# Cached keys of an attention layer turned on VectorE and through DRAM, in place of TensorE

## The chip, the cores and the metric

The kernel runs on one core of one Trainium2 chip, in fp32. The metric is the device time of one execution in microseconds (us). A core has five engines with an instruction stream each: TensorE (PE, matmuls and transposes; its weight loads are listed apart as PEld), VectorE (DVE), ScalarE (ACT), GpSimd (POOL) and SyncE (SP), which here only issues transfers. Each engine runs its own stream in order, and the streams meet at semaphores. Transfers run on 16 DMA engines beside them. SBUF and PSUM have 128 partitions.

## The reference

Four residual layers change x, 8 sequences of 128 tokens with 512 features. Layer 0 is a gated feed-forward net with low-rank adapters and then a mixture of 8 low-rank experts, layer 1 an adapter and experts, layer 3 experts chosen by language and 64 small experts. Layer 2, where the change lies, is attention with a paged cache, then experts:

```python
q = jnp.einsum('bsd,ed->bse', x, Wq).reshape(bsz, seqlen, HQ, D)   # HQ = 32, D = 128
k = jnp.einsum('bsd,ed->bse', x, Wk).reshape(bsz, seqlen, HK, D)   # HK = 8
v = jnp.einsum('bsd,ed->bse', x, Wv).reshape(bsz, seqlen, HK, D)
q, k = _rope(_rmsnorm(q, q_norm_w), pos), _rope(_rmsnorm(k, k_norm_w), pos)
kc = k_cache[block_table].reshape(bsz, L, HK, D)   # 16 pages of 32 rows: L = 512
vc = v_cache[block_table].reshape(bsz, L, HK, D)
k_all, v_all = concatenate([kc, k]), concatenate([vc, v])   # 512 cached + 128 new
scores = where(valid, einsum('bqhd,bkhd->bhqk', q, k_all) / sqrt(D), -1e30)
o = einsum('bhqk,bkhd->bqhd', softmax(scores), v_all)
out = einsum('bse,de->bsd', o.reshape(bsz, seqlen, HQ * D), Wo)
```

Here `valid` hides the cached rows at and behind `cache_seqlens`.

## The kernel before

The activations x stay in SBUF, transposed: 128 partitions, 4 chunks of features, 1024 tokens. The whole program is one launch: layers 0 and 1 take the first 329 us of the profiled execution, then attention up to about 1460 us, then the rest of layer 2 and layer 3.

**The steps of attention.** There are 32 steps n = (qd, p) (L832): the 8 key heads qd outside, 4 pairs p of sequences inside. A step handles two sequences, j = 0 and 1, each with the 4 query heads of one key head. For a step the kernel

- gathers the cached keys and values, 128 rows to an indirect DMA, four for each j and kind, on POOL's queue (`gather`, L877 to L891). The row numbers are in `kvrow`, made once from the block table (L173 to L185). Chunk c of a sequence has cached rows 128c to 128c + 127 on its partitions;
- projects the new q, k and v (`project`, with `seven`, a Strassen-like product of seven small ones: L918 matmuls, L929 and L930 VectorE, L961 the adds that give q, v and k; the last of them is k's), rotates and norms them (`rotate`, `normed`: L990 on POOL, L994, L1018, L1022 on VectorE);
- turns the cached keys so that the head's 128 features lie on the partitions (`turn_cached`, L1025 to L1034): four PE transposes of 128x128 for each j into one PSUM tile `kTc` (L1032), then a VectorE copy into the SBUF tile `kT` (L1033). `kT` is 128 x 2 x 640, and the last 128 columns of each j take the new keys, turned and copied by `turn` (L1041, L1042), which also turns q (L1047, L1049);
- computes the scores, `st`, 5 chunks of keys against 512 columns of q (L53, called from `weigh`), and their exponentials `pT` on ScalarE with the mask as bias (L1061);
- adds up the five chunks on VectorE (`added`, L1072: four adds, the last makes `part`), sums that over the keys with a PE product against ones (`sum`, L1081), takes the reciprocal (L1087), copies it to R (L1089) and spreads R with three DMAs on SP (L1091, and one more at L1092);
- multiplies with the values (`mix`: `av` on PE, L53, then `oT` on VectorE, L1103), prepares the output product (`outputs`, L900, tiles `os`), and adds the product with Wo to y (`leave`: `seven` again with the tiles `wo_one`, `wo_two`, `wo_six`, and `uo` on VectorE at L929).

**The order.** `run` (L1163 to L1230) writes the steps out by hand, three of them in flight: while step n computes its scores, step n - 1 is finished and step n + 1 is projected, rotated and turned. In the loop body of step n: scores of j = 0 and their adds; `mix` of step n - 1, j = 1; divisors of j = 0; `outputs(n - 1)`; `project(n + 1)`; `leave(n - 1)` with `rotate(n + 1)` inside it; `normed(n + 1)`; the gathers of the values for n + 1; weights for a new qd or the token sums (`tokens`, L900, tile `xs`) of step n + 2; the output weights; scores of j = 1 and their adds; `mix` of j = 0; `turn_cached(n + 1)`; the divisors of j = 1; `turn(n + 1)`; the gathers of the keys for n + 2; and the factors of new weights (L858, tiles `q_s`). Instructions that are marked `kept` stay in this order on their engine once `run` has begun; the others are moved by the framework's scheduler. Before `run`, `begin` (L1148) starts step 0 while layer 1 computes: weights, key gathers, `turn_cached(0)`, the gathers of values and of the keys of step 1, and the first factors. In that stretch layer 1's x adds (L294) and its expert routing (L238 to L266, ending in `mw_l`, which PE turns as `midTp_l` at L277) run on VectorE.

Pools: `kn` (gathered keys), `kT`, `pT` and R have two buffers for each tile, `xs`, the rotated q and k and the parts one. PSUM has three buffers for the tag "mm" (`kTc`, `kTn`, `qTp`, `sum`, most of `seven`), three for "st" and two for "av". The rotary tables' small pool `rp` lives to the end of the program.

Of the kernel before, what the change touches and what calls it, by code (L numbers as in the profile page):

```python
# [10 lines left out]
F32 = mybir.dt.float32  # L11
I32 = mybir.dt.int32
AF = mybir.ActivationFunctionType
ALU = mybir.AluOpType
# [3 lines left out]
P = 128  # L18
# [29 lines left out]
def forward(ctx: ExitStack, tc: tile.TileContext, a: dict, out: bass.AP):  # L48
# [15 lines left out]
    wop = ctx.enter_context(tc.tile_pool(name="wop", bufs=1))  # L64
    rp = ctx.enter_context(tc.tile_pool(name="rp", bufs=1))

# [22 lines left out]
    sp.dma_start(x[:, :, 512:NT], a["xT"].rearrange("(c p) t -> p c t", p=P)[:, :, 512:NT])  # L89
    second = gate_weights(1)  # L90


# [41 lines left out]
    def rows(name, n, where=const):  # L134
# [37 lines left out]

    selp = w0.tile([P, NB * 4, 4], F32, tag="selp", name="selp")  # L173
    dve.tensor_tensor(
        selp,
        table.rearrange("p (c j) -> p c j", j=4),
        block32.unsqueeze(1).to_broadcast([P, NB * 4, 4]),
        ALU.mult,
    )
    page = const.tile([P, NB * 4], F32, tag="page", name="page")  # L180
    dve.tensor_reduce(page, selp, AX.X, ALU.add)
    dve.tensor_scalar(page, page, 32.0, p_mod32, ALU.mult, ALU.add)
    kvrow = const.tile([P, NQ, NB * 4], I32, tag="kvrow", name="kvrow")
    for qd in range(NQ):
        dve.tensor_scalar(kvrow[:, qd, :], page, float(NQ), float(qd), ALU.mult, ALU.add)  # L185

# [471 lines left out]
    with psa:  # L658
# [10 lines left out]

        att = attention(tc, a, x, ident, lens, kvrow, part, ww, wop, ypool, sums, rot, ps_, c2, chunks, mm)  # L670

# [80 lines left out]
    with tc.If(redo > 0):  # L752
        sp.dma_start(x, kept)
        y2 = attention_any(tc, a, x, ident, lens, kvrow, part, ww, wop, ypool, rot, rows, chunks, mm)
        with ExitStack() as c3:
# [21 lines left out]

def attention(tc, a, x, ident, lens, kvrow, part, ww, wop, ypool, sums, rot, psa, c2, chunks, mm):

# [10 lines left out]
    ap = c2.enter_context(tc.tile_pool(name="ap", bufs=1))  # L790
    trig, straight, crossed, eps = rot

# [39 lines left out]
    steps = [(qd, p) for qd in range(NQ) for p in range(NP)]  # L832
    S = {n: {} for n in range(len(steps))}
    W, WO = {}, {}

# [40 lines left out]
    def gather(n, what):  # L876
        qd, p = steps[n]  # L877
        t = []
        for j in range(2):
            if what == "k":  # L880
                d = kvp.tile([P, 4, HD], F32, tag="kn", name=f"kn_{n}_{j}")
            else:
                d = vals[n % 2 * 2 + j]
            for c in range(4):
                i = (2 * p + j) * 4 + c
                kept(pool.indirect_dma_start(  # L886
                    out=d[:, c, :], out_offset=None, in_=kc if what == "k" else vc,
                    in_offset=bass.IndirectOffsetOnAxis(ap=kvrow[:, qd, i : i + 1], axis=0),
                ))
            t.append(d)  # L890
        S[n][what + "c"] = t  # L891

# [132 lines left out]
    def turn_cached(n):  # L1025

        s = S[n]
        kT = wk.tile([P, 2, LK], F32, tag="kT", name=f"kT_{n}")
        for j in range(2):
            ps = psa.tile([P, 512], F32, tag="mm", name=f"kTc_{n}_{j}", bufs=3)  # L1030
            for c in range(4):
                pe.transpose(ps[:, c * P : (c + 1) * P], s["kc"][j][:, c, :], ident)  # L1032
            dve.tensor_copy(kT[:, j, 0:L], ps)  # L1033
        s["kT"] = kT  # L1034

    def turn(n):
# [3 lines left out]
        for j in range(2):  # L1040
            pe.transpose(ps[:, j, :], s["k"][:, j, 0, :], ident)  # L1041
        dve.tensor_copy(s["kT"][:, :, L:LK], ps)  # L1042
        qT = []
# [9 lines left out]
    def weigh(n, j):  # L1053

        s = S[n]
        b = 2 * steps[n][1] + j
        pT = wk.tile([P, NC, REP, P], F32, tag="pT", name=f"pT_{n}_{j}")
        for c in range(NC):
            ps = psa.tile([P, REP * P], F32, tag="st", name=f"st_{n}_{j}_{c}", bufs=3)
            mm(ps, s["kT"][:, j, c * P : (c + 1) * P], s["qT"][j], True, True)  # L1060
            act.activation(  # L1061
                pT[:, c, :, :].rearrange("p i t -> p (i t)"), ps, AF.Exp,
                bias=hide[:, b, c : c + 1] if c < 4 else 0.0,
            )
        return pT
# [97 lines left out]
    def run(pool_, end, bank):  # L1163
# [12 lines left out]
        for n, (qd, p) in enumerate(steps):  # L1176
# [8 lines left out]
            if after:  # L1185
                project(after)
                leave(n - 1, lambda: rotate(after))
            elif last:
                leave(n - 1)
# [16 lines left out]
            mix(n, 0, pT)  # L1206
            if n + 1 < len(steps):
                turn_cached(n + 1)
            divisors(n, 1)
# [25 lines left out]
def rotary(tc, rp, tp, lens, part, rows, kept):  # L1235
# [43 lines left out]

    eps = rp.tile([P, 1], F32, tag="eps", name="eps")  # L1280
    pool.memset(eps, EPS_RMS)
    return (trig, straight, crossed, eps), steps(), last


def attention_any(tc, a, x, ident, lens, kvrow, part, ww, wop, ypool, rot, rows, chunks, mm):
    nc = tc.nc
# [4 lines left out]
    with ExitStack() as c2:  # L1291
        rp = c2.enter_context(tc.tile_pool(name="rp", bufs=1))
        psa = c2.enter_context(tc.tile_pool(name="psa", bufs=2, space=PSUM))

        trig, straight, crossed, eps = rot

# [9 lines left out]
        wk = c2.enter_context(tc.tile_pool(name="wk", bufs=2))  # L1306

        kc = a["k_cache"].rearrange("g s (q h) d -> (g s q) (h d)", q=NQ)
        vc = a["v_cache"].rearrange("g s (q h) d -> (g s q) (h d)", q=NQ)
# [678 lines left out]
```

## The time and the profile before

| | |
|---|---|
| median of 6 runs | 1685.52 us (1685.16 to 1690.82) |
| the profiled execution: its time, its span | 1696.47 us, 1694.7 us |
| mean granted TensorE clock | 0.991 |
| PE busy before 329 us, 329 to 1460, after 1460 | 322.25, 1071.43, 218.42 us |
| `kTc` transposes on PE, 256 | 33.2 us, 273 ns each |
| copies `kT<-kTc` on VectorE, 64 | 41.1 us, 681 ns each |
| key gathers on POOL, 256 | 269.5 us, 1053 ns each |
| R transfers on SP, 192 | 64 KB each |
| DMA traffic | 94.41 MB, mean 56 GB/s |

All times inside come from the one profiled execution; a time such as 1143.42 is counted from the start of its span. A line of the timeline gives the start, the length, the engine, the line of the program, the operation with its output and inputs by name, the tile's shape and, in brackets, how long the engine had been idle before it and what ended that. A line of the groups gives the sum of the busy time, the mean in ns, and the idle time before with its releasers. A time of 37.3 us is the usual length of an attention step.

### The profile page before, as it was taken

Reading aid. Unit: us, or ns where it says so; the run is one execution under the profiler, and the core shown is the slowest. Engines: PE = TensorE matmul, PEld = TensorE weight load, DVE = VectorE, ACT = ScalarE, POOL = GpSimd, SP = SyncE. Lnnn points to the kernel's source line nnn. Section 1 sums busy time; section 2 is a strip of 40 time slices with the busy share of each in tenths; the row PEclk is TensorE's granted clock in tenths of the full one; section 3 lists DMA queues with packets and bytes.
Section 4 is the critical chain, followed back from the end, with each engine's and each line's share of the span. In section 5 each row is a group of like instructions: output and inputs, shape, how many; then the busy total and the mean of one; then the engine's idle time right before and its main releaser. Section 6 shows DMA issues by size and latency. Waiting matters only on the chain.

```text
span 1694.7 us, 19398 instructions
## 1 busy us (share of the span) xinstructions
PE 1612.1 (95%) x6561; PEld 984.9 (58%) x6561; DVE 1073.6 (63%) x2224; ACT 563.1 (33%) x1390; POOL 818.2 (48%) x778
## 2 busy tenths in 40 slices
PE   9999999999999999999999999999999999899998
PEld 7888875555555555555555555555455555458653
DVE  4665324777777767777676767777776767663141
ACT  1111000443433344433433344443443344330110
POOL 2242025456665565656665555666566566530000
PEclk9999999999999999999999999999999999999899
DMA  8110011112121211212121211112121211202001
GB/s 291 38 44 10 1 44 53 66 38 79 45 64 44 72 35 60 74 36 65 44 77 38 67 56 51 60 39 80 40 65 44 74 35 60 84 23 79 0 13 39
DMA packets 69194, 94.41 MB, mean 56 GB/s; under 512 B 16800, under 2 KB 40544, under 8 KB 68960
## 3 DMA queue, kind: packets, MB, share of 16 engines
q1 hardware_dynamic: 50944, 56.09, 10.5%
q0 software_dynamic: 17056, 36.49, 7.0%
q8 instruction: 54, 0.88, 0.2%
q10 hardware_dynamic: 1088, 0.52, 0.1%
q14 instruction: 52, 0.43, 0.1%
HBM read 76.14 MB, written 4.33 MB: 47 GB/s over the span
## 4 chain that ended last, share of the span: by engine, by line
PE 89%; DVE 6%; issue 2%; POOL 1%; ACT 1%; another core or an unknown queue 1%; DVEq 0%; ACTq 0%; POOLq 0%
PE av L53 16%; PE st L53 15%; PE g L356 7%; PE q_six L918 7%; PE q_one L918 5%; PE wo_two L918 5%; PE q_five L918 5%; PE dn L356 4%; PE wo_one L918 3%; PE wo_six L918 3%; PE eo_l L53 2%; PE z L53 2%; PE h L1557 2%; PE qTp L1047 2%; PE o L53 2%
## 5 line engine op out<-in xcount | busy, mean ns | idle before, releaser
L53 PE MATMUL st<-qT,kT 128*128 128x512 f32 x640 | 296.1, 598 | 14.7 <-ACT pT L1061 11.6
L886 POOL DMA_INDIRECT kn<-in_k_cache,kvrow x256 | 269.5, 1053 | 80.2 <-issue 74.1
L886 POOL DMA_INDIRECT vals<-in_v_cache,kvrow x256 | 270.0, 1055 | 73.2 <-issue 45.3
L53 PE MATMUL av<-pT,vals 128*128 128x512 f32 x640 | 305.1, 600 | 0.0
L53 PEld LDWEIGHTS st<-qT,kT 128*128 128x128 f32 x640 | 116.2, 190 | 142.9 <-issue 97.3
L53 PEld LDWEIGHTS av<-pT,vals 128*128 128x128 f32 x640 | 117.4, 191 | 130.7 <-issue 130.7
L990 POOL TENSOR_TENSOR vq<-q,txq 128x512 f32<-128x512 f32 x64 | 83.4, 1324 | 224.7 <-DVE q L961 224.7
L1061 ACT ACTIVATE pT<-st,hide 128x512 f32<-128x512 f32 x256 | 168.4, 686 | 44.4 <-PE st L53 23.7
L1072 DVE TENSOR_TENSOR part<-pT 128x512 f32<-128x512 f32 x128 | 86.0, 692 | 78.5 <-ACT pT L1061 57.2
L918 PE MATMUL q_six<-q_s,xs 128*128 128x384 f32 x256 | 99.0, 506 | 13.3 <-DVE r L1087 10.5
L1049 ACT COPY qT<-qTp 128x512 f32<-128x512 f32 x64 | 37.5, 585 | 222.3 <-PE qTp L1047 164.5
L918 PE MATMUL q_one<-q,x 128*128 128x384 f32 x256 | 97.5, 504 | 3.0 <-ACT uq L926 2.6
L1130 POOL TENSOR_TENSOR y<-y,uo 128x512 f32<-128x512 f32 x32 | 44.1, 1379 | 113.0 <-DVE y L1122 113.0
L1087 DVE RECIPROCAL r<-sum 128x128 f32<-128x128 f32 x64 | 61.0, 953 | 56.2 <-PE q_one L918 32.1
L1001 ACT ACTIVATE sqq<-q 128x128 f32<-128x128 f32 x256 | 79.4, 310 | 8.3 <-DVE q L961 1.5
L918 PEld LDWEIGHTS q_six<-q_s,xs 128*128 128x128 f32 x256 | 49.2, 195 | 54.1 <-DVE r L1087 15.1
L926 ACT COPY uq<-q_one 128x384 f32<-128x384 f32 x32 | 15.3, 478 | 188.2 <-PE q_six L918 118.0
L918 PE MATMUL q_five<-q,xs 128*128 128x384 f32 x128 | 48.8, 504 | 25.0 <-DVE uq L930 25.0
L1018 DVE TENSOR_TENSOR rq<-rq,vq 128x1024 f32<-128x1024 f32 x32 | 70.4, 2199 | 1.2 <-POOL vq L990 1.2
L1103 DVE TENSOR_TENSOR oT<-av,R 128x512 f32<-128x512 f32 x64 | 44.0, 688 | 42.4 <-PE sum L1081 16.8
L918 PEld LDWEIGHTS q_one<-q,x 128*128 128x128 f32 x256 | 46.5, 193 | 36.9 <-issue 9.0
L918 PE MATMUL wo_one<-o,oT 128*128 128x256 f32 x256 | 65.8, 379 | 0.0
(387 smaller groups left out, 2873.3 us busy)
## 6 DMA issues: line engine op xcount, KB each, us to landing
R<-R SPq DMA_DIRECT2D x192, 64.0 KB
q<-in_WqT SPq DMA_DIRECT2D x8, 1024.0 KB
o<-in_WoT SPq DMA_DIRECT2D x8, 1024.0 KB
kn<-in_k_cache,kvrow POOLq DMA_INDIRECT x256
vals<-in_v_cache,kvrow POOLq DMA_INDIRECT x256
wd<-in_WdT SPq DMA_DIRECT2D x2, 1280.0 KB
wg<-in_WgT SPq DMA_DIRECT2D x9, 256.0 KB
wu<-in_WuT SPq DMA_DIRECT2D x9, 256.0 KB
```

Source lines behind the costliest of these rows:

```text
L53: pe.matmul(o, lhsT, rhs, start=start, stop=stop)
L356: pe.matmul(o, lhsT, rhs, start=start, stop=stop, skip_group_check=True)
L886: kept(pool.indirect_dma_start(out=d[:, c, :], out_offset=None, in_=kc if what == "k" else vc, in_offset=bass.IndirectOffsetOnAxis(ap=kvro ...
L918: pe.matmul(o, l[:, c, :], r[:, c, :], start=start and c == 0, stop=c == 1, skip_group_check=True)
L990: kept(pool.tensor_tensor(u[:, :, :, lo : lo + 64], t[:, :, :, hi : hi + 64], wx[:, :, lo : lo + 64].unsqueeze(2).to_broadcast(part_), ALU ...
L1001: kept(act.activation(sq, t[:, j, i, :], AF.Square, accum_out=ssq[:, j, at + i : at + i + 1]))
L1018: kept(dve.tensor_tensor(r, r, u, ALU.add))
L1061: act.activation(pT[:, c, :, :].rearrange("p i t -> p (i t)"), ps, AF.Exp, bias=hide[:, b, c : c + 1] if c < 4 else 0.0,)
L1072: kept(dve.tensor_tensor(o, l, r, ALU.add))
L1087: kept(dve.reciprocal(r, ps))
L1103: kept(dve.tensor_tensor(S[n]["oT"][:, j].rearrange("p i t -> p (i t)"), ps, S[n]["R", j], ALU.mult))
L1130: kept(pool.tensor_tensor(t, t, u.unsqueeze(1).to_broadcast([P, 2, HW]), ALU.add))
```

## The change

- `turn_cached` no longer uses PE and PSUM. VectorE transposes blocks of 32x32 inside each gathered tile: two instructions of 128x512 for a step, into a tile `kt` with one buffer. That turns each block but leaves it on its own 32 partitions. Four DMAs on SP, one for each group of 32 partitions, write `kt` to an internal DRAM tensor `turned` (128 KB each, in runs of 1 KB), and a fifth reads the 512 KB back into `kT`, 4 KB to a partition, with the blocks where they belong. All seven are marked `kept`, which holds once `run` has begun.
- The call `turn_cached(n + 1)` moves from behind `mix(n, 0)` to between `project(n + 1)` and `leave(n - 1)`; in `begin` it stays where it was.
- The keys are gathered in another order of their 32-row blocks, so that a chunk of `kT` comes out in the order that the mask expects: block b of chunk c takes the rows that were block c of chunk b. `kvrow` is made twice, for values in the old order and for keys in the new: eleven small VectorE operations more at the start.
- The new keys go to a tile of their own, `kTs`, and `weigh` reads it for the fifth chunk.
- `rp` moves to another pool context, and `eps` is made at the start; a fallback branch that this data does not take makes its own rotary angles.

```diff
+    kvrow = {}
+    for what, order in (("v", "p (b c j) -> p b c j"), ("k", "p (b j c) -> p b c j")):
+        selp = w0.tile([P, NB, 4, 4], F32, tag="selp", name="selp_" + what)
...
+    turned = nc.dram_tensor("turned", (len(steps), 4, 32, 4, 8, 32), F32, kind="Internal").ap()
...
-                    in_offset=bass.IndirectOffsetOnAxis(ap=kvrow[:, qd, i : i + 1], axis=0),
+                    in_offset=bass.IndirectOffsetOnAxis(ap=kvrow[what][:, qd, i : i + 1], axis=0),
...
     def turn_cached(n):
 
         s = S[n]
-        kT = wk.tile([P, 2, LK], F32, tag="kT", name=f"kT_{n}")
+        t = wk.tile([P, 4, 8, 32], F32, tag="kt", name=f"kt_{n}", bufs=1)
+        kT = wk.tile([P, 4, 8, 32], F32, tag="kT", name=f"kT_{n}")
         for j in range(2):
-            ps = psa.tile([P, 512], F32, tag="mm", name=f"kTc_{n}_{j}", bufs=3)
-            for c in range(4):
-                pe.transpose(ps[:, c * P : (c + 1) * P], s["kc"][j][:, c, :], ident)
-            dve.tensor_copy(kT[:, j, 0:L], ps)
+            kept(dve.transpose(
+                t[:, :, 4 * j : 4 * j + 4, :], s["kc"][j].rearrange("p c (b d) -> p b c d", b=4)
+            ))
+        for q in range(4):
+            kept(sp.dma_start(
+                turned[n, :, :, q].rearrange("b i m d -> i b m d"), t[32 * q : 32 * q + 32]
+            ))
+        kept(sp.dma_start(kT, turned[n].rearrange("b i a m d -> (b i) a m d")))
         s["kT"] = kT
 
     def turn(n):
...
-        dve.tensor_copy(s["kT"][:, :, L:LK], ps)
+        s["kn"] = wk.tile([P, 2, P], F32, tag="kTn", name=f"kTs_{n}")
+        dve.tensor_copy(s["kn"], ps)
...
-            mm(ps, s["kT"][:, j, c * P : (c + 1) * P], s["qT"][j], True, True)
+            mm(ps, s["kT"][:, c, 4 * j : 4 * j + 4, :] if c < 4 else s["kn"][:, j, :], s["qT"][j], True, True)
...
             if after:
                 project(after)
+            if n + 1 < len(steps):
+                turn_cached(n + 1)
+            if after:
                 leave(n - 1, lambda: rotate(after))
...
             mix(n, 0, pT)
-            if n + 1 < len(steps):
-                turn_cached(n + 1)
             divisors(n, 1)
```

## The prediction

> **What bounds the kernel now.** I read first the page's shares of busy time and the chain that ended last:
>
> ```profile
> PE 1612.1 (95%) x6561; PEld 984.9 (58%) x6561; DVE 1073.6 (63%) x2224; ACT 563.1 (33%) x1390; POOL 818.2 (48%) x778
> ...
> PE 89%; DVE 6%; issue 2%; POOL 1%; ACT 1%; another core or an unknown queue 1%; DVEq 0%; ACTq 0%; POOLq 0%
> ```
>
> PE is the bound, and VectorE holds most of the rest of the chain. So work taken from PE can shorten the span, but only where PE does not then wait for VectorE. Second, the groups by shape, for what the change takes away:
>
> ```profile
> L1033 DVE COPY kT<-kTc 128x512 f32<-128x512 f32 x64 | 41.1, 681 | 0.0
> ...
> L1032 PE MATMUL kTc<-ident,kn 128*128 128x128 f32 x256 | 33.2, 273 | 0.0
> ...
> L1081 PE MATMUL sum<-part,ones 128*32 128x128 f32 x512 | 27.3, 284 | 6.0 <-DVE part L1072 5.9
> ```
>
> The third line says who is late already: `sum` waits for VectorE's `part` for 5.9 us in all. So, third, the timeline of PE and of VectorE in an ordinary step (start, length, operation):
>
> ```profile
> 1139.99 3.60 PE L53 MATMUL av<-pT,vals 128*128 128x512 f32 x8
> 1143.42 1.04 PE L1032 MATMUL kTc<-ident,kn 128*128 128x128 f32 x8
> 1144.39 0.43 PE L1081 MATMUL sum<-part,ones 128*32 128x128 f32 x8
> ```
>
> ```profile
> 1129.34 0.28 DVE L961 TENSOR_TENSOR k<-q_six,uq 128x128 f32<-128x128 f32 x1
> 1131.65 0.42 DVE L929 TENSOR_TENSOR uo<-wo_two,uo 128x256 f32<-128x256 f32 x1 [2.04 <-PE wo_two L918]
> ...
> 1142.71 0.69 DVE L1072 TENSOR_TENSOR part<-part,part 128x512 f32<-128x512 f32 x1
> 1143.51 0.69 DVE L1072 TENSOR_TENSOR part<-part,pT 128x512 f32<-128x512 f32 x1
> ```
>
> The reader is to see that the last `part` add ends at 1144.20, 0.78 us after kTc's start: kTc fills a time in which `sum` could not have run. VectorE is busy without a gap from `uo` at 1131.65 to that add; its last rest is the 2.04 us before `uo`.
>
> **Part 1: the transposes leave PE.** Eight of them hold PE 0.97 us a step (1143.42 to 1144.39). Without them `sum` starts when `part` is done. PE follows VectorE's end by 0.05 us (uq ends 1126.06, q_five starts 1126.11) to 0.15 us (342.75, 342.90), so `sum` comes 0.83 to 0.93 us after kTc's old start: the step gains about 0.1. I compared the two times in all 31 steps that have kTc before `sum`. In 21 it is as here (0.77 to 0.78): 21 x 0.1 = 2.1 us. In 7, which have no `tokens` adds there, `part` ends 0.69 us before kTc's start, and the whole 0.97 is won: 6.8. One (at 1489 us) ends 0.14 before: 1.0. In two (346, 1407) `part` comes 2.6 to 2.7 after kTc's start: nothing. Sum: **-9.9 us**, of the 33.2 that kTc is busy. The two PSUM copies (1.28 us a step) stand behind that add and ahead of `kTn`'s copy; PE's next reader of them has slack, so I give their removal nothing.
>
> **Part 2: the transposes on VectorE.** The order in which the changed program issues them puts both between the `k` add and `uo`, in the 2.04 us gap. The nearest row is one instruction:
>
> ```profile
> L107 DVE STREAM_TRANSPOSE within<-ramp x1: 205/205/205, 2.3 to 2.3; 128x32 f32<-128x32 f32 x1
> ```
>
> Adds go from 0.42 (256 columns) to 0.69 us (512), 1.05 ns a column. At that rate 128x512 is 0.205 + 480 x 1.05 ns = 0.71 us, and the pair 1.35 us, which the gap covers with 0.7 to spare. The bounds: at 0.205 each (no growth) 0.4; at 16 x 205 ns each, 6.6, which is 4.5 a step over the gap. I take 0.71, since every VectorE row here with 512 columns lies between 0.68 and 0.97. If they are longer than 1.02 each, all that stands from `uo` to `part` is late by the excess, and `sum` with it. The instruction's wait is for `kn`; its gathers' last issue is 5.8 to 13.7 us before the `k` add's end, so it should not wait in steady steps.
>
> The Trainium skill, page "VectorE: DVE Perf Modes", sections "The three transpose paths" and "Rules for kernel authors", speaks against the move: it advises TensorE for 128x128 where PSUM will do, and gives VectorE 311 ns for 128x128 in bf16. By that page the pair would be an estimated 8 x 0.311 = 2.5 us, 0.45 over the gap, and 22 such steps would cost 10 us, all that part 1 wins; no run here shows bf16.
>
> **Part 3: the way through DRAM.** SP issues four writes of 128 KB and one read of 512 KB a step. The issues are priced by those of R (1.77 us for three, 0.59 each), a landing by R too (issue 1526.3, reader oT at 1528.6: 2.3 us), the read's data by Wq (1.5 MB in 705.75 to 712: near 250 GB/s, 2.1 us). From the `k` add's end: 1.35 + 2.4 + 2.3 + 0.6 + 2.3 + 2.1 = 11 us. The next step's first `st` starts 18.0 to 18.2 us after that end: 7 us of slack. Where SP also carries weights, they stand between writes and read and leave 4 to 5. Bounds: no less than zero; a landing of twice 2.3 still fits in ordinary steps. If it is late, each us counts 31 times. Queued behind SP's waiting read are the second R group of the step, due 14 us later, and weights for the next `qd`. Traffic grows by 2 x 16.8 MB on 94.4, at a mean DMA share of 18%: nothing. The keys' other order and its eleven small VectorE operations fit into a 2.14 us wait near 21 us: nothing. `kTn` in a tile of its own: the same copy.
>
> **Part 4: step 0.** Here the same two instructions stand elsewhere on VectorE: among the factors of the first weights, ahead of an `x` add and of layer 1's route chain (L241 to L266), in the order of the program. Their data is late:
>
> ```profile
> 254.74 1.64 POOL L886 DMA_INDIRECT kn<-in_k_cache,kvrow  x1 [0.17 <-issue]
> ...
> 264.56 0.94 POOL L886 DMA_INDIRECT kn<-in_k_cache,kvrow  x1 [0.31 <-issue]
> 265.81 0.94 POOL L886 DMA_INDIRECT vals<-in_v_cache,kvrow  x1 [0.30 <-issue]
> ```
>
> ```profile
> 265.02 0.69 DVE L266 TENSOR_TENSOR mw_l<-mid_l,e_l 128x512 f32<-128x512 f32 x1
> ```
>
> ```profile
> 269.02 0.60 PE L277 MATMUL midTp_l<-ident,mw_l 128*128 128x128 f32 x4
> ```
>
> POOL cannot issue these gathers before 254.74 (it makes the rotary tables until then), so the second tile is there at about 265.5 + 1.7 = 267.2, when the chain had been done at 265.71. After: second transpose to 267.9, `x` add to 268.5, factors to 270.4, route chain 4.66 us (261.05 to 265.71) to 275.1; PE's transposes start at 275.2 for 269.02: **+6.2 us**. A PE idle of 2.7 us at 660 was followed by a granted clock of 0.69 and 0.50, with q_six at 2.80 for 1.45 us and q_one at 1.95; I add the 1.85. Off goes kTc at 290.98, 0.9. Step 0 together: **+7.2 us**. Bounds: 0, if PE has other work ready there (the `eo_l` matmuls behind, which are not in the issue order), and 8.1.
>
> **Sum**, against the profiled execution's own 1696.47 us: -9.9 + 7.2 = -2.7, 1693.8. The median of the runs shown is 1685.52, 0.65% under the profiled one; in its terms **1683 us**, own range 1679 to 1688. About 0.2% (3.4 us) is what a measurement can tell from no change, so this stands on the edge.
>
> **Rivals.**
> Likeliest, chance 0.40: as above, 1683.
> Second, 0.25: the gain is larger. For it: PE's order is written by a scheduler, and step 0 may have other matmuls to put ahead, then -9.9 + 0 - 0.9 and 1675. If VectorE's chain also shortens by the 1.28 us of copies, so that `part` comes as early as kTc went, all 31 steps give 0.97, 30.1, less the 7.2: 1663. Against it: `part` is tied to VectorE's busy stretch, in which the copies are not.
> Third, 0.35, slower: the two transposes, at the place between `k` add and `uo`, take over 2.04 us. It decides from 1.02 us each. At twice the adds' rate, 2.1 ns a column, each is 1.21, the pair 2.42, and 0.38 x 22 steps gives +8: 1691. At 1.5 each, 3.0 and 0.96 x 22 = +21: 1704. For it: the one row here is 6.4 ns a column, and VectorE has no slack behind. Against it: 205 ns is what 32-column operations of other kinds take too (0.18 to 0.20). A kT that lands late, at a weight step or everywhere, would show the same sign with the wait at `st` instead.
> That the change doesn't do what it says (kTc's work kept on PE) is excluded by the order of its instructions: 256 transposes fewer on PE.
>
> **How the numbers follow.** Predicted: 1683. Range 1662 to 1705: from the second case's far end to the third's at 1.5 each; beyond it lies a pair of up to 6.6 us (+100 us) at under one in ten. Chances: faster by over 0.2% (under 1682.1): the second case and 0.16 of the first; within 0.2%: 0.20 of the first, 0.04 of the third; slower: 0.04 and 0.31. That is 0.41, 0.24, 0.35.
>
> **What would show it.** Part 1: in 22 steps PE's idle before `sum` names `part`, at some 0.8 us; in 7 none. Part 2: STREAM_TRANSPOSE 128x512 at 0.7 us and still an idle before `uo`. Part 3: no idle before `st` that names kT's DMA. Part 4: VectorE idle until `kn` lands near 262 to 267, and PE idle 6 us before `midTp_l` near 269, at a lower clock behind it. It is wrong if the transposes exceed 1.02 us, if `st` waits for the read, or if the lags of the signals behind the first `sum` (recip starts at 1120.32, 2.4 us after that `sum` ends) change with the order; why these are so long the trace does not tell, and I leave them as they are.

## The result and the profile after

The changed kernel takes **1699.94 us** (median of 20 runs, 1688.6 to 1707.64), the kernel before 1685.17 us beside it (46 runs, 1673.94 to 1695.51): a ratio of **1.0085**, 95% interval 1.0071 to 1.01. (All ratios below are to the kernel before, beside it on the same chip, with the interval in brackets.) It is 14.8 us slower, where 2 us faster had been forecast. The profiled execution after took 1698.12 us, span 1696.0, mean granted clock 0.982. The profiled execution of before that the prediction read (1696.47 us) lies above all 46 of these runs, so the two pages differ by less than the medians; a second one of before, at 1684.43 us (e5_before2 below), is what I compare with.

Shares of busy time and the chain that ended last, after:

```profile
PE 1591.2 (94%) x6305; PEld 960.5 (57%) x6305; DVE 1076.2 (63%) x2235; ACT 564.8 (33%) x1390; POOL 818.3 (48%) x778
...
PE 74%; DVE 17%; POOL 2%; issue 2%; DMA 2%; another core or an unknown queue 2%; ACT 1%; SPq 0%; ACTq 0%; DVEq 0%; POOLq 0%
```

PE lost 21 us of work, and part of the chain passed from PE (89% before, 74% now) to VectorE (6% before, 17% now). The groups by shape say where PE waits for it:

```profile
L1038 DVE STREAM_TRANSPOSE kt<-kn 128x512 f32<-128x512 f32 x64 | 41.6, 687 | 10.3 <-DMA kn<-in_k_cache,kvrow_k 10.1
L1094 PE MATMUL sum<-part,ones 128*32 128x128 f32 x512 | 27.3, 285 | 19.4 <-DVE part L1085 19.2 <-issue 0.2
```

The transposes take 0.687 us each, and `sum` waits 19.4 us for `part`, where it was 6.0. An ordinary step, VectorE and then PE (start, length, operation, idle before it):

```profile
1131.23 0.28 DVE L968 TENSOR_TENSOR k<-q_six,uq 128x128 f32<-128x128 f32 x1
1131.43 1.29 DVE L1038 STREAM_TRANSPOSE kt<-kn 128x512 f32<-128x512 f32 x2
1133.55 0.42 DVE L936 TENSOR_TENSOR uo<-wo_two,uo 128x256 f32<-128x256 f32 x1 [0.83 <-PE wo_two L925]
```

```profile
1146.15 0.43 PE L1094 MATMUL sum<-part,ones 128*32 128x128 f32 x8 [0.67 <-DVE part L1085]
```

The pair lies inside the rest before `uo`, and PE waits 0.67 us where it turned keys before. Up to here the steady step does what was forecast. The loss shows in the steps that take over new output weights, where VectorE makes the factors `o_s`. One of them, PE, VectorE, ScalarE and POOL:

```profile
1115.24 0.43 PE L1094 MATMUL sum<-part,ones 128*32 128x128 f32 x8
1115.60 1.56 PE L925 MATMUL q_one<-q,x 128*128 128x384 f32 x4
...
1118.28 1.45 PE L925 MATMUL q_five<-q_s,xs 128*128 128x384 f32 x4
1123.73 1.65 PE L925 MATMUL q_six<-q_s,xs 128*128 128x384 f32 x4 [4.00 <-DVE r L1100]
1125.17 2.77 PE L925 MATMUL q_one<-q,x 128*128 128x384 f32 x4
```

```profile
1117.06 0.69 DVE L1116 TENSOR_TENSOR oT<-av,R 128x512 f32<-128x512 f32 x1 [3.07 <-PE sum L1094]
1122.72 0.96 DVE L1100 RECIPROCAL r<-sum 128x128 f32<-128x128 f32 x1 [4.97 <-remote]
```

```profile
1122.83 0.48 ACT L933 COPY uq<-q_one 128x384 f32<-128x384 f32 x1 [10.31 <-remote]
```

```profile
1119.32 0.95 POOL L893 DMA_INDIRECT kn<-in_k_cache,kvrow_k  x1 [0.30 <-issue]
```

`sum` ends at 1115.67 and `q_one` at 1117.16, yet the reciprocal that reads the one starts at 1122.72 and the copy that reads the other at 1122.83: 7.05 and 5.67 us late, together, with a releaser that the profile cannot name ("remote"; in the chain 4.95 us of "an unknown queue"). Two engines that resume within 0.11 us of each other point to PE's completion signals, not to either engine. The trace's records of the semaphore that PE raises say the same: its steps for the ends of `sum`, `q_one`, `q_six` and `q_five` (1115.67, 1117.15, 1118.44 and 1119.73) stand at 1122.70, 1122.76, 1122.82 and 1122.88, while VectorE's own semaphore steps at 1117.76, 0.01 us behind `oT`'s end. POOL's row is the last of sixteen gathers that it issues without a break. PE then sits idle for 4.00 us, and `q_one` behind that takes 2.77 us for the usual 1.45 (granted clock 0.50 there): the step is 41.1 us long, most others 35.9 to 36.6. These lags, 2.35 us long in an ordinary step before, are what my prediction left "as they are".

### The profile page after: what moved, and what is told of

It reads as the page before. It is cut to its first block, busy times and chain, and to the rows that moved or that the text cites. A ratio compares the mean times of both kernels' runs of the same rounds, so it can differ in the third digit from the quotient of the medians.

```text
span 1696.0 us, 19220 instructions
## 1 busy us (share of the span) xinstructions
PE 1591.2 (94%) x6305; PEld 960.5 (57%) x6305; DVE 1076.2 (63%) x2235; ACT 564.8 (33%) x1390; POOL 818.3 (48%) x778
## 4 chain that ended last, share of the span: by engine, by line
PE 74%; DVE 17%; POOL 2%; issue 2%; DMA 2%; another core or an unknown queue 2%; ACT 1%; SPq 0%; ACTq 0%; DVEq 0%; POOLq 0%
PE st L53 10%; PE av L53 10%; PE q_six L925 7%; PE g L362 7%; PE q_one L925 5%; PE q_five L925 5%; PE wo_two L925 4%; PE dn L362 4%; DVE part L1085 4%; DVE rq L1025 3%; PE wo_one L925 3%; PE wo_six L925 2%; PE z L53 2%; DVE xs L907 2%; PE sum L1094 2%
## 5 line engine op out<-in xcount | busy, mean ns | idle before, releaser
L893 POOL DMA_INDIRECT vals<-in_v_cache,kvrow_v x256 | 273.5, 1068 | 73.3 <-issue 58.2
L893 POOL DMA_INDIRECT kn<-in_k_cache,kvrow_k x256 | 266.5, 1041 | 79.9 <-issue 77.6
L53 PE MATMUL av<-pT,vals 128*128 128x512 f32 x640 | 296.0, 593 | 0.0
L53 PE MATMUL st<-qT,kT 128*128 128x512 f32 x512 | 239.4, 599 | 4.0 <-DMA kT<-turned 4.0
L53 PEld LDWEIGHTS st<-qT,kT 128*128 128x128 f32 x512 | 93.6, 193 | 99.9 <-issue 80.3
L925 PE MATMUL q_one<-q,x 128*128 128x384 f32 x256 | 103.3, 529 | 0.0
L1062 ACT COPY qT<-qTp 128x512 f32<-128x512 f32 x64 | 37.5, 586 | 169.0 <-PE qTp L1060 152.8
L1025 DVE TENSOR_TENSOR rq<-rq,vq 128x1024 f32<-128x1024 f32 x32 | 70.3, 2198 | 1.2 <-POOL vq L997 1.2
```

What stands on the lines that cost most here:

```text
L53: pe.matmul(o, lhsT, rhs, start=start, stop=stop)
L893: kept(pool.indirect_dma_start(out=d[:, c, :], out_offset=None, in_=kc if what == "k" else vc, in_offset=bass.IndirectOffsetOnAxis(ap=kvro ...
L925: pe.matmul(o, l[:, c, :], r[:, c, :], start=start and c == 0, stop=c == 1, skip_group_check=True)
L1025: kept(dve.tensor_tensor(r, r, u, ALU.add))
```

## The experiments

The theory after the result: **A**, the loss lies in lags of PE's signals while POOL issues gathers in a row, which the new order lengthens. The rivals: **B**, the start costs what part 4 said and steady steps gain nothing; **C**, VectorE's chain is the bound, for its new place or for the transposes' length; **D**, keys arrive late through DRAM. "Step" is the time between the starts of `kTn` on PE in the trace.

**e1_start**: the transposes of step 0 wait, in program order, behind layer 1's x adds and route chain (`add_to_x` keeps its order while `hold` is set).

```diff
-        outs0(1, (0, 1), large_bank)
+        hold.append(1); outs0(1, (0, 1), large_bank); hold.clear()
...
-            kept(dve.transpose(
+            tc.keep_in_program_order(dve.transpose(
```

> The changed kernel with one thing put back in its place: in step 0 the two VectorE transposes are held behind the x adds and the route chains of layer 1, so that VectorE no longer waits for the first key gathers at 255 to 269 us. Theory S (the start costs what the trace shows, 5.6 us of PE idle and the slow clock behind it): 6 to 9 us less than the changed kernel. Rival (the start is made up for later, since PE only catches up with another wait): less than 2 us off.

Measured 1691.59 us, ratio 1.0022 [0.9991, 1.0053], since before took 1690.0 in these runs. That is 8.3 us less than the changed kernel's median, and about 11 by the two ratios, of which this one is uncertain by 0.3%. `midTp_l` no longer waits. From layer 1's first `midTp_l` to the first `kTn` the trace has 82.3 us, for 87.3 in the changed kernel and 79.7 in e5_before2; the other runs with this edit have 80.6 to 81.0. So the start is worth 5 to 7 us, near the 7.2 of part 4, and it is not the only loss: the long steps stay at 41.1.

**e2_nokeys**, **e3_before_nokeys**: no key gathers from step 2 on (every step uses step 1's keys), in the changed kernel and in the one before.

```diff
+        if what == "k" and n > 1:
+            S[n]["kc"] = S[1]["kc"]
+            return
```

> The changed kernel without the key gathers of steps 2 to 31 (240 of 256 indirect DMAs left out; every step uses the keys of step 1, so that the attention is computed on other keys). Theory G (PE's completion signals behind the first sum of a step are held up while POOL issues a step's sixteen gathers, and come about 2 us after the last): the lag from sum to reciprocal, 7.0 us in the steps with new output factors and 0.3 to 1.5 in the others, goes to under 0.3 in all, the 41.1 us steps become 36 or less, and the time falls by 35 to 60 us. Rival D (the way of the keys through DRAM or the VectorE transposes hold PE's signals up): the lags stay, the time moves by less than 5 us.

> The kernel before, again without the key gathers of steps 2 to 31 (all use the keys of step 1). Theory G: its lag of 2.35 us and more goes too, and with it the 1.54 us wait at q_five in each step: 40 to 60 us less than before. Rival D: the lag in the kernel before has another cause than gathers, and it stays; the time moves by less than 5 us.

Measured 1622.10 (ratio 0.9615 [0.9563, 0.9667]) and 1629.65 (0.9667 [0.9613, 0.972]). Without the gathers the changed kernel takes 78 us less, more than the 35 to 60 that I expected, and the kernel before 55 less (60 against the 1690.0 beside it). The order turns round: without them the changed kernel is 7.5 us the faster, with them 14.8 the slower. Steps are 35.17, each fourth 34.43, after; they are 35.50 before, 36.4 to 36.9 with new weights. The lag behind the first `sum` is at most 0.3 us in both. B falls as the whole story.

**e4_hwkeys**: the same bytes of keys, issued by SP as plain transfers of a fixed choice of rows.

```diff
+                if what == "k" and n > 1:
+                    kept(sp.dma_start(d[:, c, :], rows_k[i % 16 * P : i % 16 * P + P, qd, :]))
+                    continue
                 kept(pool.indirect_dma_start(
```

> The changed kernel with the keys of steps 2 to 31 loaded by plain DMAs on SP, eight a step with the same bytes, from fixed rows instead of the rows of the block table. Theory G in the form that POOL's issuing of indirect DMAs does the harm: as without key gathers, 35 to 60 us less than the changed kernel. G in the form that the bytes or the packets of 512 B do it: lags stay near 7 us in the steps with new output factors, the time within 10 us of the changed kernel. Rival D: as the second.

Measured 1625.6, ratio 0.9657 [0.9598, 0.9717], with steps of 35.17 and 34.43. The bytes cost little (1625.6 for 1622.1); their issue on POOL costs the time.

**e5_before2** (the kernel before once more, one run), **e6_novals** (no value gathers from step 2 on: the scores meet step 1's values) and **e7_nofactors** (the output weights' factors are not made anew; old tiles stand in).

```diff
+        if what == "v" and n > 1:                       # e6_novals
+            S[n]["vc"] = None
+            return
...
-                WO[qd].factors()                        # e7_nofactors
+                WO[qd].B = WO[qd].B[:3] + WO[qd].B[:3] + WO[qd].B[:1]
```

> The kernel before, profiled once more. Theory G: the lag behind the first sum is not noise of one profile: about 2.3 us in ordinary steps again, and larger and unequal in the steps behind new weights or output factors. If the profile of before was an odd one: other values in ordinary steps.

> The changed kernel without the value gathers of steps 2 to 31 (the cached values of steps 0 and 1 serve for all), with all key gathers. Theory G1 (the harm grows over an unbroken block of sixteen gathers): the eight key gathers alone leave lags under 1 us, time 1630 to 1660 us. Theory G2 (it is the key gathers' place beside the first sum and q products that counts): lags as in the changed kernel, 7 us behind new output factors, time within 10 us of it. Theory D: as G2.

> The changed kernel without VectorE's four factor operations on new output weights in seven steps (their products then use plain quarters of the weights). If these operations, together with the gathers, make the lag of 7 us: it falls to the 0.3 to 1.5 us of other steps and the 41.1 us steps to about 36.3, 7 x 4.8 = 34 us less than the changed kernel. If the lag belongs to the step's place in the gathers' order (two sequences' pages) and not to VectorE: 41 us steps stay, less than 5 us off.

e5_before2: 1684.43 us, steps mostly 37.3, and the lag in an ordinary one (PE, then VectorE; `sum` ended at 1107.80):

```profile
1107.37 0.43 PE L1081 MATMUL sum<-part,ones 128*32 128x128 f32 x8
```

```profile
1107.47 0.69 DVE L1103 TENSOR_TENSOR oT<-av,R 128x512 f32<-128x512 f32 x1 [0.50 <-PE av L53]
1110.20 0.96 DVE L1087 RECIPROCAL r<-sum 128x128 f32<-128x128 f32 x1 [2.03 <-PE q_one L918]
```

e6_novals: 1616.26 us, one run, less than the 1630 to 1660 that G1 gave. PE and VectorE at the same place (`sum` ended at 1105.48):

```profile
1105.05 0.43 PE L1097 MATMUL sum<-part,ones 128*32 128x128 f32 x8
```

```profile
1105.16 0.69 DVE L1119 TENSOR_TENSOR oT<-av,R 128x512 f32<-128x512 f32 x1 [1.36 <-PE av L53]
1105.77 0.95 DVE L1103 RECIPROCAL r<-sum 128x128 f32<-128x128 f32 x1
```

Without the value gathers the lag is 0.3 us although all key gathers are there: neither kind alone does it. Whether it takes sixteen in a row, or sixteen in a step however they stand, these runs do not tell, since each halves both. e7_nofactors: 1669.26 us, one run; the steps with new output factors fall from 41.1 to between 36.6 and 37.5, with lags of 0.3 to 1.5 us (two of the last, at 40.2 and 40.4, stay). So the four VectorE adds of the factors take part in the longest lags; how, the runs do not tell.

**e8_place**: the kernel before without key gathers, with its PE transposes at the changed kernel's place.

```diff
+            if n + 1 < len(steps):
+                turn_cached(n + 1)
             if after:
                 leave(n - 1, lambda: rotate(after))
...
             mix(n, 0, pT)
-            if n + 1 < len(steps):
-                turn_cached(n + 1)
```

> The kernel before without the key gathers of steps 2 to 31, and the PE transposes with their two copies moved to the changed kernel's place (between the q products and the output products). Against the same kernel at the old place (steps of 35.50 us, and 36.4 with new weights): if the old place hid kTc under PE's wait for part (prediction, part 1), PE now waits there and pays kTc elsewhere: about 0.9 more a step, 36.4. If the place is free: 35.5.

1638.0 us, one run: steps 36.2, each fourth 35.47, against 35.50 at the old place. PE work put there costs 0.7 us a step, where I expected 0.9, so a place ahead of `uo` is paid for; VectorE's transposes use it free only because VectorE rested there.

The runs from here on fell on two other chips. There the kernel before takes **1621 us** (medians 1621.02, 1620.94, 1621.21 and 1621.33) at the same granted clock (0.994; 0.993 in e5_before2), so each is told against before on its own chip.

**e9_split**: e1_start, and the eight key gathers move from behind the steps' end to behind `rotate`, so that POOL issues 8 and 8 with its tensor work between.

```diff
-                leave(n - 1, lambda: rotate(after))
+                leave(n - 1, lambda: (rotate(after), gather(n + 2, "k") if n + 2 < len(steps) else None))
...
             if n + 2 < len(steps):
-                gather(n + 2, "k")
+                if not after:
+                    gather(n + 2, "k")
```

**e10_facs**: e1_start, and the output factors of a new `qd` are made one step later, behind `added(n, 0)`. **e11_double**: e1_start, no key gathers from step 2 on, each transpose made twice. **e12_before_split**: the kernel before with its PE transposes, and the gathers split in the same way (`kn` with four buffers).

```diff
+            if n > 1 and p == 1:                        # e10_facs; the call at the step's end goes
+                WO[qd].factors()
...
-        for j in range(2):                              # e11_double, in turn_cached
+        for j in (0, 1, 0, 1):
```

> The changed kernel with step 0's transposes held back and with the block of sixteen gathers split: the key gathers of step n + 2 now stand on POOL between the rotations and the y adds of step n + 1, ahead of the y adds and the value gathers, and their rows are free since the VectorE transposes come early. Nothing is left out. Theory G1 (an unbroken block of sixteen gathers, ending beside the first sum, holds PE's signals up): lags under 0.5 us, steps of 35.2 us, 1612 to 1640 us, faster than both kernels. Rival (it is the number of gathers in a step, however they stand): lags stay, within 10 us of the changed kernel with the start mended (1691).

> The changed kernel with step 0's transposes held back and the four factor operations on new output weights moved from the end of a step to behind the first adds of the next one, all else as in the changed kernel. Theory F (these operations beside the gathers make the lag of 7 us; they may run elsewhere): the eight 41.1 us steps become 37 to 38, 1655 to 1670 us. Rival (any VectorE work beside the gathers does it, wherever it stands): 41 us steps stay, near 1691.

> The changed kernel with the start mended, without the key gathers of steps 2 to 31 (all use the keys of step 1), and with each VectorE transpose made twice. Two more take 1.3 us a step; the gap before uo is 2.04 us wide and the first pair fills 1.3. Prediction, part 2: 0.55 us of it stick out and `part`, and with it the second sum, comes later by that in each step: steps of 35.7 us instead of 35.17. If the gap takes both pairs: 35.17. If all of it counts: 36.5.

> PE transposes as in the kernel before, with the gathers split in the same way; for that the gathered keys have two buffers more, in room that the smaller rotary pool leaves. Nothing is left out. Theory G1: the 1.5 us stalls at q_five go here too, steps of 35.5 (36.4 with new weights), 1620 to 1640 us. So the two ways of turning the keys can be compared without the gathers' harm: the changed one should be 0.74 us a step better, 10 to 25 us. Rival: lags stay, 1685.

e9_split: 1605.81, ratio **0.9900** [0.9884, 0.9917]. e12_before_split: 1620.79, ratio 0.9997 [0.9987, 1.0007]. So on one chip, with the gathers split in both and the start mended, VectorE's way of turning the keys is 15.0 us the better, inside the 10 to 25 that I expected. Of the theories on the lags e9_split, e10_facs and e12_before_split tell nothing, since no signal is late on this chip. e10_facs: 1617.44, 0.9977 [0.9966, 0.9988]. e11_double: 1619.79, one run; steps 35.37 for 35.17, where I expected 35.7, and `uo` directly behind four transposes, 2.60 us behind `k`'s start for 2.32 with two:

```profile
1076.09 2.48 DVE L1041 STREAM_TRANSPOSE kt<-kn 128x512 f32<-128x512 f32 x4
1078.49 0.39 DVE L939 TENSOR_TENSOR uo<-wo_two,uo 128x256 f32<-128x256 f32 x1
```

So 0.28 us stick out of the gap, not 0.55, and twice the length costs 0.20 us a step: the transposes as they are cost none that shows, and C holds only for the rest of VectorE's chain. What the split takes from that chain, in the groups of the changed kernel and then of e9_split:

```profile
L1025 DVE TENSOR_TENSOR rq<-rq,vq 128x1024 f32<-128x1024 f32 x32 | 70.3, 2198 | 1.2 <-POOL vq L997 1.2
```

```profile
L1025 DVE TENSOR_TENSOR rq<-rq,vq 128x1024 f32<-128x1024 f32 x32 | 39.2, 1226 | 1.2 <-POOL vq L997 1.2
L1094 PE MATMUL sum<-part,ones 128*32 128x128 f32 x512 | 27.3, 285 | 9.3 <-DVE part L1085 9.1
```

In the changed kernel that `rq` takes 2198 ns, and POOL adds `y<-y,uo` beside it (e13_after):

```profile
1123.06 1.38 POOL L1143 TENSOR_TENSOR y<-y,uo 128x512 f32<-128x512 f32 x1 [2.61 <-DVE y L1135]
```

```profile
1123.22 2.29 DVE L1025 TENSOR_TENSOR rq<-rq,vq 128x1024 f32<-128x1024 f32 x1
```

With the gathers between, POOL's add starts 9 us behind `rq`, `rq` takes 1226 ns, `sum` waits no more in ordinary steps, and steps are 34.43 (35.36 with new weights). The Trainium skill, page "SBUF — State Buffer", section "Who interferes with whom", says that a VectorE instruction with two SBUF inputs contends with a GpSimd instruction that reads SBUF; the 0.97 us between the two rows agrees. Before has the shorter `rq` too when its gathers are split, but gains only 0.18 us a step by it (35.50 to 35.32) and nothing in its time; its `sum` hardly waited for `part` (5.1 us in all in e16_before3).

**e13_after** (the changed kernel unaltered), **e14_split_again** (e9_split again), **e15_noway** (e1_start, no key gathers and no way through DRAM from step 2 on: `st` reads step 1's keys, the transposes stay).

```diff
+        if n > 1:                                       # e15_noway, in turn_cached behind the transposes
+            s["kT"] = S[1]["kT"]
+            return
```

> The changed kernel itself once more, since the last runs of before, on the chip they got, took 1621 us instead of 1685 to 1690. Theory G1 with a condition (PE's signals are held up by the gathers on some chips and not on others): where before takes 1621, the changed kernel shows no lag of 7 us, its steps with new output factors take 35.2 us, and it takes before's time less 22 (steps) plus 12 (step 0 and step 1), 1608 to 1618: faster than before. Where before takes 1685: 1700 again. Rival (the loss behind new output factors belongs to the change itself): 41.1 us steps wherever it runs, 1640 or more beside a before of 1621.

> The version with the start mended and the gathers split, again beside before. Theory G1: 1600 to 1612 us whether before takes 1621 or 1685 here, since it has no block of sixteen gathers to be held up by. Rival: where before takes 1685, this takes 60 more as well, 1660 to 1670.

> The changed kernel with the start mended, without key gathers from step 2 on and without the way through DRAM from step 2 on (every step uses the turned keys of step 1; the VectorE transposes stay, and their output goes nowhere). Prediction, part 3 (the way through DRAM is hidden but for first steps): the steps stay at 35.17 and 34.43 us. Rival (its writes, reads and SP's waits cost in each step): they get shorter by over 0.2 us.

e13_after: 1623.2 (10 runs), ratio **1.0018** [1.0006, 1.0029]: within 0.2% on this chip. The lags went, as the theory says, but the 1608 to 1618 that I expected was missed: the changed kernel is not the faster here either. Its shares and chain, and PE and VectorE at the place where the signals were late:

```profile
PE 1566.3 (97%) x6305; PEld 954.9 (59%) x6305; DVE 1075.9 (66%) x2235; ACT 564.7 (35%) x1390; POOL 819.4 (51%) x778
...
PE 77%; DVE 15%; DMA 3%; POOL 3%; issue 2%; ACT 1%; SPq 0%; ACTq 0%; DVEq 0%; POOLq 0%
```

```profile
1106.82 0.43 PE L1094 MATMUL sum<-part,ones 128*32 128x128 f32 x8
```

```profile
1106.93 0.69 DVE L1116 TENSOR_TENSOR oT<-av,R 128x512 f32<-128x512 f32 x1 [1.35 <-PE av L53]
1107.54 0.95 DVE L1100 RECIPROCAL r<-sum 128x128 f32<-128x128 f32 x1
```

The reciprocal starts 0.29 us behind `sum`'s end, and "unknown queue" is gone from the chain. e14_split_again: 1605.73, 0.9901 [0.9877, 0.9926]. e15_noway: 1614.45, one run, with the same 35.17 and 34.43. D falls for steps 2 and on.

**e16_before3** (before, one run) and **e17_best**: e9_split, and step 1's keys are turned ahead of the loop, behind `turn(0)`.

```diff
         turn(0)
+        turn_cached(1)
         running.append(True)
...
-            if n + 1 < len(steps):
+            if n + 1 < len(steps) and n:
                 turn_cached(n + 1)
```

> The kernel before, profiled once more, to have its trace where it takes 1621 us. Theory G1 with the condition (a chip either holds PE's signals up beside gathers or does not): if its time here is near 1621, lags under 0.3 us behind the first sum, steps of 35.3 to 35.5 us; if it is near 1685, lags of 2.4 and steps of 37.3. Rival (the chips differ in something else, such as the clock or the DMAs): 1621 with lags of 2.4 us.

> The split version with step 1's cached keys turned before step 0 begins, too, so that their way through DRAM (10.1 us from the transposes' end at 348.1 to st at 358.2 us) no longer makes st wait 4.75 us. Nothing is left out. Theory: 4 to 5 us less than the split version (1605.8): 1600 to 1602. Rival (VectorE pays the two transposes elsewhere before step 0): within 1.5 us of it.

> The best version once more, for the case that before takes 1685 us here. Theory G1 (only an unbroken block of sixteen gathers is held up by): 1600 to 1610 us then too. Rival (the split blocks are held up by as well): 1650 to 1670. Where before takes 1621, it tells nothing new: 1601.

e16_before3: 1620.12, steps 35.50 (35.63 with new weights), lags of 0.3 us at most behind the first `sum`. e17_best: 1601.18, ratio **0.9869** [0.9844, 0.9894], the best of all; e18_best_again, the same kernel, 1601.19, 0.9873 [0.9852, 0.9894]. It was meant for a chip on which signals come late, and fell on one where they do not.

The traces show one more difference between the chips. On the one with late signals they lack records of semaphore steps, and only near gathers: of the steps by VectorE and ScalarE in the changed kernel's trace, 625 of 1100 are recorded while POOL issues gathers and up to 2 us behind them, and 1737 of 1737 at other times; in e13_after none is missing. With eight gathers in a row (e6_novals) 512 of 755 are recorded. So something on that chip holds up or loses signals or their records beside gathers, in rows of eight too. Whether the recording itself takes part in the lags was not tested.

## Why the prediction was wrong

By the medians the change costs 14.8 us where before takes 1685, and 2.3 (1623.2 less 1620.9) where it takes 1621. So I put **12.5 us of the loss down to the late signals**, and 2.3 stand against my sum of -2.7. The traces split much the same, with the 12.5 in steps 2 to 30 (e5_before2 and after, spans 1682.5 and 1696.0; e16_before3 and e13_after, 1618.2 and 1620.4, from two chips on which before takes 1621):

| change by the stretch, us | predicted | signals late | signals in time |
|---|---|---|---|
| start to the first `kTn` | +7.2 | +7.2 | +9.8 |
| step 0, step 1 | 0, 0 | +0.8, +4.1 | +0.8, +4.0 |
| steps 2 to 30 | -9.9 | -3.6 | -16.1 |
| last step and behind | 0 | +5.0 | +3.7 |
| sum | -2.7 | +13.5 | +2.2 |

**The step that failed** is the last sentence of the forecast: "the lags of the signals behind the first `sum`", which I left "as they are". They were in the profile, 2.4 us long, with a stall of `q_five` behind them; steps of 37.3 us in place of 35.50, and some longer ones, are what before pays over its 1621 us: 62.4 in steps 2 to 30 (e5_before2 less e16_before3). The changed kernel pays 74.9 there (after less e13_after). I named the change of order as a danger and gave it no price and no chance. The new order left ordinary lags at 0.3 to 1.5 us, but made 7.0 of them in six of the seven steps with new output factors and 5.4 in the last: steps 2 to 30 gain 3.6 us in place of 16.1. Shown: the lag goes if half of the sixteen gathers goes (e2, e3, e6) or if SP issues the same bytes (e4), shrinks without the factors (e7), and is absent on two other chips (e13, e16). That it is PE's signals that come late is read from two engines resuming together and from the records of PE's semaphore; the mechanism under it is open, and so is why a chip shows it.

The late signals are not all. Where they come in time the sign is still wrong: what I put at nothing, step 0, step 1, the last step and 2.6 us ahead of part 4's stretch, adds 11.1 us, and steps 2 to 30 gain only 6.2 more than my -9.9. That the measured 1699.94 lies inside my range is luck: the range reached so far only for transposes of 1.5 us each, which did not come.

**Part 1** had the right size where I looked. From `wo_two` to `sum` a quiet step takes 14.73 us in e16_before3 and 14.59 in e13_after, 0.14 for my 0.1:

```profile
1077.01 1.89 PE L918 MATMUL wo_two<-o_s,os 128*128 128x256 f32 x8
...
1091.74 0.42 PE L1081 MATMUL sum<-part,ones 128*32 128x128 f32 x8
```

```profile
1082.01 1.89 PE L925 MATMUL wo_two<-o_s,os 128*128 128x256 f32 x8
...
1096.60 0.43 PE L1094 MATMUL sum<-part,ones 128*32 128x128 f32 x8 [0.67 <-DVE part L1085]
```

Each fourth step wins 1.07 for my 0.97. From `sum` to the next `wo_two`, where I had not looked, another 0.20 went (20.77 to 20.57); I did not trace what it was. In 21 steps that is 4.2 of the 6.2 us between -16.1 and -9.9.

**Part 2** was right: 0.687 us for 0.71, and 0.83 us of rest left before `uo` for 0.7. One of its grounds was not: single VectorE operations of 128x512 in the trace of before run from 0.43 to 1.65 us, not from 0.68 to 0.97. The third rival's mechanism (transposes over 1.02 us) did not happen; the sign it forecast came from elsewhere. My worry by the Trainium skill, page "VectorE: DVE Perf Modes", section "The three transpose paths" (311 ns for 128x128 in bf16, so an estimated 1.24 us for four side by side) differs from the 0.687 measured here in fp32; the measurement decides.

**Part 3** was right from step 2 on (e15_noway changes no step) and wrong in step 1. PE there, after:

```profile
364.08 5.27 PE L53 MATMUL st<-qT,kT 128*128 128x512 f32 x8 [4.04 <-DMA kT<-turned]
```

That is 9.4 us behind the transposes' end. In e9_split the way takes 10.1 us, from their end at 348.10 to `st` at 358.23, 1.1 of it while SP still issues R; I had said 11 with the transposes in it:

```profile
346.80 1.30 DVE L1038 STREAM_TRANSPOSE kt<-kn 128x512 f32<-128x512 f32 x2
```

```profile
358.23 6.67 PE L53 MATMUL st<-qT,kT 128*128 128x512 f32 x8 [4.75 <-DMA kT<-turned]
```

Only the slack was wrong: I took 18 us from steady steps, but in step 0 the loop projects nothing, `turn_cached(1)` stands behind `divisors(0, 0)`, and the scores could start 5.4 us behind the transposes' end (358.23 - 4.75 - 348.1). That is the 4.0 us of step 1, which e17_best and e18_best_again win back (1605.81 to 1601.18 and 1601.19); in e17_best `st` follows `qTp` with no idle:

```profile
355.74 3.60 PE L53 MATMUL st<-qT,kT 128*128 128x512 f32 x8
```

**Part 4** was right in mechanism and place. VectorE waits for `kn` twice, and PE for VectorE:

```profile
263.75 0.71 DVE L1038 STREAM_TRANSPOSE kt<-kn 128x512 f32<-128x512 f32 x1 [6.36 <-DMA kn<-in_k_cache,kvrow_k]
...
269.07 0.71 DVE L1038 STREAM_TRANSPOSE kt<-kn 128x512 f32<-128x512 f32 x1 [3.77 <-DMA kn<-in_k_cache,kvrow_k]
```

```profile
276.85 1.09 PE L283 MATMUL midTp_l<-ident,mw_l 128*128 128x128 f32 x4 [5.63 <-DVE e_l L270]
```

PE's idle was 5.63 us here and 7.49 in e13_after, for 6.2; the second tile lands some 2 us later than I reckoned (269.0 for 267.2), because POOL begins these gathers at 256.81 for 254.74. From layer 1's first `midTp_l` to the first `kTn` the changed kernel takes 7.6 us more in the one pair of traces and 7.2 in the other, for my 7.2. Ahead of that stretch, where I had put the eleven small operations at nothing, the two traces with signals in time differ by 2.6 of the +9.8: the kernel before reaches that first `midTp_l` at 245.2 us, the changed one at 247.8. Over all traces the two lie at 245.2 to 248.7 and at 247.5 to 251.1, and e12_before_split, which has the new operations too, at 246.8. What makes the difference was not traced.

**The last step** was not priced at all. Of its +3.7, 1.8 stand in a wait of the output's transposes `y2T` for POOL's last `y` adds (e16_before3, then e13_after):

```profile
1419.01 1.17 PE L1604 MATMUL y2T<-ident,y 128*128 128x128 f32 x6 [1.14 <-POOL y L1130]
```

```profile
1419.38 1.37 PE L1621 MATMUL y2T<-ident,y 128*128 128x128 f32 x6 [2.92 <-POOL y L1143]
```

The rest I did not trace. But e8_place, which still turns the keys on PE, has +4.0 here as well (207.1 us for 203.1 in e3_before_nokeys, a trace each) and +0.8 in step 0: so these two terms go with the new place of the call, not with VectorE or DRAM.

## What to carry to other kernels

An idle time whose releaser the profile cannot name, or names as an instruction that ended long ago, is a cost that an edit of the order can double: price it like any other term, or let it set the width of the range. Work moved from the bounding engine to the next one pays only in full when that one's chain is shortened too: here 0.33 us a step alone, for the 0.97 that the transposes held PE, and 1.07 once POOL's adds no longer ran beside VectorE's two-input product (0.89 against before with its own gathers split). And slack that is read from steady steps must be read again in the first and the last.

## What the runs showed of the hardware

- While POOL issues sixteen indirect gathers in a row, results of PE reach VectorE and ScalarE 2.4 us late in ordinary steps of the kernel before, and 7.0 in some of the one after; with eight in a step, or eight by SP and eight by POOL, 0.3. This on one chip and not on two others, at the same granted clock, where the kernel before takes 64 us less (1685.2 to 1621), 62.4 of them in steps 2 to 30. Whether breaking the row in two (e9_split) mends it there was not measured.
- VectorE turns a 128x512 tile of fp32 in blocks of 32x32 in 0.687 us, as long as a copy of that size (681 ns), and the way of 512 KB through DRAM takes 9.4 (after) to 10.1 us (e9_split) from the last transpose to the first reader.
- `rq`, a 128x1024 VectorE product of two SBUF tiles, takes 1226 ns with no POOL add beside it (e9_split) and 2198 ns beside a POOL add that reads SBUF (after).
